# VectorE and TensorE in program order in the first stage of a two-layer adaLN kernel

## The chip, the cores and the metric

The kernel runs on one core of a Trainium2 chip. The time is the device time of one execution in microseconds (us), the median of three runs. A profile of one further execution shows every instruction.

## What is computed

Two layers follow each other on `x` of 8 batches, 512 tokens and 256 channels, all in float32. Each layer has an attention part and an expert part, and both are modulated (adaLN): shift, scale and gate come from a small product of `silu(c)`.

```python
h = _layernorm(x) * (1 + ca) + sa
x = x + ga * attention(h)
h = _layernorm(x) * (1 + cb) + sb
x = x + gb * experts(h)
```

In layer 0 the attention is a linear one with 16 heads of 64: `q` and `k` have one number a head, and running sums over the tokens replace the softmax.

```python
cos_KV = jnp.cumsum(cos_k * V, axis=1)
sin_KV = jnp.cumsum(sin_k * V, axis=1)
heads = cos_q * cos_KV + sin_q * sin_KV
denom = cos_q * cumsum(cos_k) + sin_q * cumsum(sin_k) + EPS
heads = heads / denom
out = jnp.einsum('deh,bthe->btd', W_O, heads)
```

Its experts are 4, two for each token, with `silu(x w1) * (x w3)` and `w2`. Layer 1 has a softmax attention among 16 positions of small heads, and 8 experts, one for each token.

## The kernel before

**The stages.** The batches of layer 0 are in two halves, `first` (0 to 3) and `second` (4 to 7). The first stage runs the attention of batches 0 to 3, routes their tokens to experts, makes the table of expert tiles (`table`), and begins the attention of batch 4. Then the expert tiles of the first half start (`line.run(m0, ...)`): from there on TensorE works on expert tiles (`up` L753, `down` L768), and the attention of later batches and of layer 1 is put between them.

**Attention of one batch (`attend0`).** Before a batch's steps, `prepare0(b)` makes its rows in three parts. The first is `norm_T`: `stats` on VectorE (four `bn_stats`, an ACT Sqrt at L185, a reciprocal and one Newton step), the normalised `xn` on ScalarE (L198), transposes on TensorE (L217), modulation on ScalarE (`hT`, L204), the product `pq` (L336), Tanh and four Sin on ScalarE. It then goes on with `before` on GpSimd, the products `pd` (L358, L359), the denominators on VectorE (L362 to L369), transposes (L372) and row copies on ScalarE (L376). The last part is one VectorE product (L379), and the rows are written to DRAM from GpSimd's queue. The steps of batch b call the parts of batch b+1 at j = 0, 3 and 5.

The batch itself has 8 steps j of two heads each (`heads0`). SyncE (SP) loads `ratio` and `factor`, rows spread over the partitions, in four DMAs of 256 KB (3 and 2 buffers). TensorE makes `pv` (L398). VectorE runs two scans (L404), a product (L407) and an addition (L409) to `hd`. After the eight steps `out0` multiplies by `W_O`: four tiles of 128 tokens, `poa` (L415), each of eight products over all `hd`. VectorE multiplies each tile by the gate (`ra`, L226) and GpSimd adds it to `x` (L227).

**Routing (`Moe.route`).** For a batch whose attention is done: `stats` and `normed` again, transposes (L499), logits `pl` (L504), transposes back (`prow`, L512), `z` on VectorE (L520), an Exp on ScalarE, two maxima with their indices (`first_max`), prefix sums, a product `pk` with a triangle (L562), slot positions (L575), and eight indirect DMAs from GpSimd's queue that scatter the rows to slots (L579). The generator stops five times on the way. `table` then counts the tiles.

**What sets the order.** The code is generators: `weave(main, side)` runs one piece of `side` after each piece of `main`. In the first stage, batch 0's steps are woven with loads and the modulation of layer 1 (`rest`), and those of batch b with the routing of batch b-1 and then the re-ordering of a weight (`wq_steps`, ScalarE copies). That is the program's order. It is not the order of the engines: the framework schedules the traced instructions and puts each engine's queue in the order in which it expects their inputs to be ready. At run time an engine's queue is worked through as written. Manual dependencies and `issue_after` are the only marks on that order.

PSUM has four buffers for `pv` and expert products (`ps_h`), two for `poa` (`ps_o`), and two for all small products and transposes (`ps_m`).

Of the kernel before, what the change touches and what calls it, by code (L numbers as in the profile page):

```python
# [9 lines left out]
F32 = mybir.dt.float32  # L10
# [18 lines left out]
def kernel(  # L29
# [99 lines left out]


# [3 lines left out]
    def modulation(l, c, wmod, mp):  # L134
# [4 lines left out]
        for n in range(3):  # L139
# [3 lines left out]
            for kk in range(KD):  # L143
                nc.tensor.matmul(pr[:B, :], sc[:, kk, :], wm[:, kk, :], start=(kk == 0), stop=(kk == KD - 1))
            rows = mp.tile([B, 2, D], F32, tag="rows", name=f"rows{l}_{n}", bufs=1)
            nc.vector.tensor_copy(rows.rearrange("b c d -> b (c d)"), pr[:B, :])
            for i in range(2):
                j = 2 * n + i
                if j % 3 == 1:
                    nc.vector.tensor_scalar(rows[:, i], rows[:, i], 1.0, None, ALU.add)  # L150
                elif j % 3 == 2:
                    sgn = mp.tile([B, D], F32, tag="sgn", name=f"sgn{l}_{j}", bufs=1)
                    nc.vector.tensor_scalar(sgn, rows[:, i], 0.0, 2.0, ALU.is_ge, ALU.mult)
                    mag = mp.tile([B, D], F32, tag="mag", name=f"mag{l}_{j}", bufs=1)
                    nc.scalar.activation(mag, rows[:, i], AF.Abs)
                    nc.vector.tensor_scalar(mag, mag, GATE_MIN, None, ALU.max)
                    nc.vector.scalar_tensor_tensor(rows[:, i], sgn, -1.0, mag, ALU.add, ALU.mult)
            by_channel = [i for i in range(2) if (2 * n + i) % 3 != 2]
            pm = ps_m([P, len(by_channel), KD, B], f"pmT{l}_{n}")
            for m, i in enumerate(by_channel):  # L160
                for k in range(KD):
                    nc.tensor.transpose(pm[:, m, k, :], rows[:, i, k * P : (k + 1) * P], ident[:B, :B])
            at = (0, 2, 3)[n]
            nc.vector.tensor_copy(modT[l][:, at : at + len(by_channel)], pm)
# [10 lines left out]
    def stats(b, nm):  # L175
# [3 lines left out]
        for t in range(NT):  # L179
            nc.vector.bn_stats(st[:, t, :], x[b][:, t, :])  # L180
            nc.vector.bn_aggr(mv[:, t, :], st[:, t, :])
        v = wk.tile([P, NT], F32, tag="var", name=f"var{nm}")
        nc.vector.tensor_scalar(v, mv[:, :, 1], LN_EPS, None, ALU.add)
        r = wk.tile([P, NT], F32, tag="rstd", name=f"rstd{nm}")
        nc.scalar.activation(r, v, AF.Sqrt)  # L185
        nc.vector.reciprocal(r, r)
        n = wk.tile([P, NT], F32, tag="newton", name=f"newton{nm}")
        nc.vector.scalar_tensor_tensor(n, r, -0.5, r, ALU.mult, ALU.mult)
        nc.vector.tensor_mul(n, n, v)
        nc.vector.scalar_tensor_tensor(r, n, 1.5, r, ALU.add, ALU.mult)  # L190
        return mv, r

    def normed(b, mv, r, dst, nm):

        sh = wk.tile([P, NT], F32, tag="sh", name=f"sh{nm}")
        nc.vector.scalar_tensor_tensor(sh, mv[:, :, 0], -1.0, r, ALU.mult, ALU.mult)
# [11 lines left out]
    def norm_T(l, b, dst):  # L208


        mv, r = stats(b, f"{l}_{b}")
        xn = wk.tile([P, NT, D], F32, tag="xn", name=f"xn{l}_{b}", bufs=1)
        normed(b, mv, r, xn, f"{l}_{b}")
        for k in range(KD):
            pt = ps_m([P, NT, P], f"pt{l}_{b}_{k}")
            for t in range(NT):
                nc.tensor.transpose(pt[:, t, :], xn[:, t, k * P : (k + 1) * P], ident)  # L217
# [5 lines left out]
    def residual(po, gate, b, t, name):  # L223

        tmp = wk.tile([P, D], F32, tag="tmp", name=name, bufs=2)
        nc.vector.tensor_mul(tmp, po, gate)  # L226
        nc.gpsimd.tensor_tensor(x[b][:, t, :], x[b][:, t, :], tmp, ALU.add)  # L227
# [101 lines left out]
    def prepare0(b):  # L329
# [4 lines left out]
        for t in range(NT):  # L334
            for k in range(KD):
                nc.tensor.matmul(  # L336
# [21 lines left out]
        nc.tensor.matmul(pd, tri, c, start=True, stop=False)  # L358
        nc.tensor.matmul(pd[:, 1:], ones, before, start=False, stop=True)  # L359
        ab = tr[:, :, 2]  # L360
        rd = ap.tile([P, NT, H], F32, tag="rd", name=f"rd{b}", bufs=1)
        nc.vector.tensor_mul(ab, sq, pd)  # L362
        nc.vector.tensor_add(rd, ab[:, :, 0, :], ab[:, :, 1, :])
        nc.vector.tensor_scalar(rd, rd, DEN_EPS * math.sin(2 * ALPHA), None, ALU.add)
        nc.vector.reciprocal(rd, rd)
        nc.vector.reciprocal(tr[:, :, 1], c)
        for i in range(2):
            nc.vector.tensor_mul(ab[:, :, i], sq[:, :, i], rd)
        nc.vector.tensor_mul(ab, ab, c)  # L369
        pt = ps_m([3 * 2 * H, NT, P], f"ptr{b}")  # L370
        for t in range(NT):
            nc.tensor.transpose(pt[:, t, :], tr[:, t].rearrange("p a i h -> p (a i h)"), ident)  # L372
# [6 lines left out]
        nc.vector.tensor_mul(rows[1][:, 1:], rows[1][:, 1:], rows[0][:, : S - 1])  # L379
# [5 lines left out]
    def heads0(b, j):  # L385
# [11 lines left out]
        for k in range(KD):  # L397
            nc.tensor.matmul(  # L398
                pv, wv_sb[:, k, j * P : (j + 1) * P], hTs[b][:, k, :],
                start=(k == 0), stop=(k == KD - 1),  # L400
            )
        u = ap.tile([P, 2, S], F32, tag="u", name=f"u{b}_{j}", bufs=2)
        for i in range(2):
            nc.vector.tensor_tensor_scan(  # L404
                out=u[:, i], data0=w[0][:, i], data1=pv, initial=0.0, op0=ALU.mult, op1=ALU.add
            )
        nc.vector.tensor_mul(u, u, w[1])  # L407
        hd = ap.tile([P, S], F32, tag="hd", name=f"hd{b}_{j}", bufs=9)
        nc.vector.tensor_add(hd, u[:, 0], u[:, 1])  # L409
        return hd  # L410

    def out0(b, t, hds, ga):
        po = ps_o(f"poa{b}_{t}")
        for j in range(NJ):
            nc.tensor.matmul(  # L415
                po, hds[j][:, t * P : (t + 1) * P], wo_sb[:, j, :], start=(j == 0), stop=(j == NJ - 1),
            )
        residual(po, ga, b, t, f"ra{b}_{t}")

    def attend0(b):  # L420

# [3 lines left out]
        for j in range(NJ):  # L425
            hds.append(heads0(b, j))
            if j in (0, 3, 5):
                next(nxt, None)
            yield
        for t in range(NT):  # L430
            out0(b, t, hds, ga)
        yield

    hTs = {}
# [10 lines left out]
    def first_max(v, E, m, o, name):  # L445


        nc.vector.tensor_reduce(m, v, AX.X, ALU.max)
        nc.vector.tensor_tensor(o, v, bcast(m, E), ALU.is_equal)
        nc.vector.tensor_mul(o, o, desc[:, :E].unsqueeze(1).to_broadcast([P, NT, E]))  # L450
        k = wk.tile([P, NT], F32, tag="rm", name=f"k{name}", bufs=4)
        nc.vector.tensor_reduce(k, o, AX.X, ALU.max)
        nc.vector.tensor_tensor(o, o, bcast(k, E), ALU.is_equal)

    class Moe:
# [19 lines left out]
        def route(self, i):  # L475
# [9 lines left out]
            h0 = ht[0]  # L485
            mv, r = stats(b, f"f{bm}")
# [9 lines left out]
            for k in range(KD):  # L496
                pt = ps_m([P, NT, P], f"ptr{bm}_{k}")
                for t in range(NT):
                    nc.tensor.transpose(pt[:, t, :], h0[:, t, k * P : (k + 1) * P], ident)  # L499
                by_channel(l, 2, k, b, hT[:, k], pt.rearrange("p t q -> p (t q)"))  # L500
            pl = ps_m([P, NT, E], f"pl{bm}")
            for t in range(NT):
                for k in range(KD):
                    nc.tensor.matmul(  # L504
# [3 lines left out]
            for t in range(0, NT, 2):  # L508
                pb = ps_m([P, 2, D], f"prow{bm}_{t}")
                for q in range(2):  # L510
                    for k in range(KD):
                        nc.tensor.transpose(  # L512
# [7 lines left out]
            nc.vector.tensor_tensor(z, pl, b_sb.unsqueeze(1).to_broadcast([P, NT, E]), ALU.add)  # L520
# [6 lines left out]
            if l == 0:  # L527
                s = wk.tile([P, NT], F32, tag="rs", name=f"s{b}")
                nc.vector.tensor_reduce(s, z, AX.X, ALU.max)
                nc.vector.tensor_tensor(z, z, bcast(s, E), ALU.subtract)  # L530
                nc.scalar.activation(z, z, AF.Exp)
                nc.vector.tensor_reduce(s, z, AX.X, ALU.add)
                nc.vector.reciprocal(s, s)
                nc.vector.tensor_mul(z, z, bcast(s, E))
                first_max(z, E, m[0], ch[0], f"a{b}")
                nc.vector.scalar_tensor_tensor(z, ch[0], -2.0, z, ALU.mult, ALU.add)
                first_max(z, E, m[1], ch[1], f"b{b}")
                now = wk.tile([P, NT, E], F32, tag="now", name=f"now{bm}", bufs=2)
                nc.vector.tensor_add(now, ch[0], ch[1])
                nc.vector.tensor_add(s, m[0], m[1])  # L540
                nc.vector.reciprocal(s, s)
                for c in range(C):
                    nc.vector.tensor_mul(ht[c][:, :, D + 1], m[c], s)
            else:
                nc.scalar.activation(z, z, AF.Exp, scale=-1.0)
                nc.vector.tensor_scalar(z, z, 1.0, None, ALU.add)
                nc.vector.reciprocal(z, z)
                first_max(z, E, m[0], ch[0], f"c{b}")
                now = ch[0]
                nc.vector.tensor_copy(ht[0][:, :, D + 1], m[0])  # L550

            pre = fp.tile([P, NT + 1, E], F32, tag=f"pre{E}", name=f"pre{bm}", bufs=3)
            if i == 0:
                nc.vector.memset(pre[:, 0], 0.0)
            else:
                nc.vector.tensor_copy(pre[:, 0], self.run_)
            for t in range(NT):
                nc.vector.tensor_add(pre[:, t + 1], pre[:, t], now[:, t])
# [3 lines left out]
            nc.tensor.matmul(pk, tri, now, start=True, stop=False)  # L562
            nc.tensor.matmul(pk, ones, pre[:, :NT], start=False, stop=True)
            yield
            rank = wk.tile([P, NT, E], F32, tag="rank", name=f"rank{bm}", bufs=2)
            nc.vector.tensor_tensor(
# [4 lines left out]
            for c in range(C):  # L571
                nc.vector.tensor_mul(at, ch[c], rank)  # L572
                p_ = fp.tile([P, NT], I32, tag=f"pos{c}", name=f"pos{c}_{bm}", bufs=3)
                with nc.allow_low_precision("whole numbers"):
                    nc.vector.tensor_reduce(p_, at, AX.X, ALU.add)  # L575
# [16 lines left out]
        def table(self):  # L592
# [3 lines left out]
            nc.tensor.matmul(pn, ones, self.run_, start=True, stop=True)  # L596
            n = wk.tile([P, E], F32, tag="cnt", name=f"cnt{nm}", bufs=1)
            nc.vector.tensor_copy(n, pn)
            past_ = fp.tile([1, E1], I32, tag="pasts", name=f"past{nm}", bufs=2)[:, :E]
            nc.vector.scalar_tensor_tensor(past_, n[0:1], 1.0, cbase[0:1, :E], ALU.add, ALU.add)  # L600
            self.past = past_
            cmp_ = wk.tile([P, E, TH], F32, tag="cmp", name=f"cmp{nm}", bufs=1)
            nc.vector.tensor_tensor(
# [3 lines left out]
            nc.vector.tensor_reduce(nt, cmp_, AX.X, ALU.add)  # L607
            upto = wk.tile([P, E, E], F32, tag="upto", name=f"upto{nm}", bufs=1)
            nc.vector.tensor_tensor(
# [3 lines left out]
            nc.vector.tensor_reduce(end, upto, AX.X, ALU.add)  # L613
            base = wk.tile([P, E], F32, tag="base", name=f"base{nm}")
            nc.vector.tensor_sub(base, end, nt)
            full = [P, J, E]

            def of_tile(v, op, rows, dst, name, weigh=None):

                t_ = wk.tile(full, F32, tag="past", name=f"{name}{nm}", bufs=1)  # L620
                nc.vector.tensor_tensor(
                    t_, bcast(rows[:, :J], E), v.unsqueeze(1).to_broadcast(full), op
                )
                if weigh is not None:
                    nc.vector.tensor_tensor(t_, t_, weigh.unsqueeze(1).to_broadcast(full), ALU.mult)
                nc.vector.tensor_reduce(dst, t_, AX.X, ALU.add)
# [4 lines left out]
            nc.vector.tensor_scalar(self.tab[:, 0], which, float(E - 1), None, ALU.min)  # L631
            nc.vector.tensor_scalar(nt, nt, -1.0, float(CAP), ALU.mult, ALU.add)
            skip = wk.tile([P, J], F32, tag="skip", name=f"skip{nm}", bufs=1)
            of_tile(end, ALU.is_ge, iota, skip, "rows", weigh=nt)
            nc.vector.tensor_add(skip, skip, iota[:, :J])
            nc.vector.tensor_scalar(self.tab[:, 1], skip, float(P), float(E * CAP * P), ALU.mult, ALU.min)

            lim = wk.tile([P, E], F32, tag="lim", name=f"lim{nm}", bufs=1)
            nc.vector.scalar_tensor_tensor(lim, base, float(P), n, ALU.mult, ALU.add)
# [3 lines left out]
            nc.vector.tensor_sub(self.used, self.used, skip)  # L643
            self.rest = fp.tile([P, JMAX], F32, tag="rest", name=f"rest{nm}", bufs=2)[:, :J]
            nc.vector.scalar_tensor_tensor(
# [5 lines left out]
        def keep(self, end):  # L651
# [3 lines left out]
            nc.vector.tensor_scalar(  # L655
# [8 lines left out]
            for t, v in zip(k, (self.tab, self.used, self.rest)):  # L664
                nc.vector.tensor_copy(t, v[..., over])
# [602 lines left out]
```

## Time and profile before

| | us |
|---|---|
| median of three runs | 2013.6 (2009.74 to 2014.16) |
| the profiled execution | 1998.39 |
| its span, first to last instruction | 1996.7 |
| PE busy in the span | 1757.0 (88%) |
| DVE busy | 1258.1 (63%) |
| ACT busy | 728.8 (37%) |
| POOL busy | 594.9 (30%) |
| first scan of batch 0 | at 40.7 |
| first scan of batch 4 | at 274.4 |
| first expert matmul | at 328.9 |

PE is TensorE, PEld its weight loads, DVE VectorE, ACT ScalarE, POOL GpSimd, SP SyncE; `SPq` is SP's queue of DMAs. A row of the timeline gives start, length, engine, line, operation, out <- in, and how many instructions it merges (`x4`); a float32 matmul counts as two. In square brackets stands the engine's idle time before it, and what ended that. A row of the waits gives who waited, for whom, the total in us, how often and the longest. Granted clock (`PEclk`) is in tenths of full speed in the slices, and as a fraction in the windows.

### The profile page before, as it was taken

How to read it: one execution, taken by the hardware profiler on the slowest of the kernel's cores; microseconds unless marked ns; L12 is line 12 of the kernel's file. 1: busy time of each engine (PE TensorE's matmuls, PEld its weight loads, DVE VectorE, ACT ScalarE, POOL GpSimd, SP SyncE). 2: the span in 40 equal slices, each digit the busy share in tenths (PEclk: the TensorE clock that was granted, in tenths of full speed). 3: DMA queues.
4: the chain of work that ended last, by engine and by line, in shares of the span. 5: the costliest groups of instructions: out<-in, count | busy, mean ns of one | idle time of the engine just before them, and what ended most of it. 6: DMA issues, size and time to landing. Idle time of an engine off the chain costs nothing. (4 is left out here: it accounts for less than half of the span.)

```text
span 1996.7 us, 32445 instructions
## 1 busy us (share of the span) xinstructions
PE 1757.0 (88%) x11336; PEld 1536.1 (77%) x11336; DVE 1258.1 (63%) x2200; ACT 728.8 (37%) x1384; POOL 594.9 (30%) x564
## 2 busy tenths in 40 slices
PE   6686776999999999989999999997969988898895
PEld 3354435888888889888999889897868877787784
DVE  4786886344433441235999999623499999986200
ACT  5052212231312212226343334622645646454221
POOL 1033132121121121233435444213345464433210
PEclk9797986999999999989999999998989999899898
DMA  7977777899898996896777668799644665579795
GB/s 225 213 206 204 181 185 252 238 315 301 260 307 276 310 332 224 315 323 214 240 246 230 215 229 280 239 320 312 201 132 144 208 202 181 188 241 330 254 348 168
DMA packets 328535, 488.60 MB, mean 245 GB/s; under 512 B 24016, under 2 KB 184048, under 8 KB 327728
## 3 DMA queue, kind: packets, MB, share of 16 engines
q1 hardware_dynamic: 313840, 445.17, 71.6%
q0 software_dynamic: 14528, 41.31, 5.6%
q8 instruction: 92, 1.51, 0.3%
q14 instruction: 75, 0.61, 0.1%
HBM read 446.40 MB, written 45.27 MB: 246 GB/s over the span
## 5 line engine op out<-in xcount | busy, mean ns | idle before, releaser
L753 PE MATMUL p<-xT,w 128*128 128x128 f32 x6144 | 767.5, 281 | 29.7 <-DMA w<-in_W_dram 16.3
L753 PEld LDWEIGHTS p<-xT,w 128*128 128x128 f32 x6144 | 747.0, 198 | 44.4 <-issue 20.1
L768 PE MATMUL po<-w_d,g 128*128 128x256 f32 x1952 | 477.8, 385 | 26.7 <-DVE g L760 16.8
L768 PEld LDWEIGHTS po<-w_d,g 128*128 128x128 f32 x1952 | 355.3, 193 | 78.8 <-DVE g L760 20.5
L783 POOL DMA_INDIRECT ys<-y,to x122 | 153.9, 1261 | 658.3 <-ACT xT L728 420.8
L758 ACT ACTIVATE g<-p 128x512 f32<-128x512 f32 x244 | 145.8, 598 | 462.8 <-PE p L753 432.8
L760 DVE TENSOR_TENSOR g<-g,p 128x512 f32<-128x512 f32 x140 | 95.8, 685 | 274.0 <-PE p L753 253.9
L404 DVE TENSOR_TENSOR_SCAN u<-ratio,pv 128x512 f32<-128x512 f32 x128 | 149.6, 1204 | 57.1 <-PE pv L398 51.4
L989 POOL TENSOR_TENSOR far<-q 128x1024 f32<-128x1024 f32 x64 | 133.1, 2081 | 120.2 <-DVE pr L1047 75.8
L398 PE MATMUL pv<-hT,wv_sb 128*128 128x512 f32 x256 | 138.1, 661 | 33.6 <-DVE u L404 27.5
L415 PE MATMUL poa<-wo_sb,hd 128*128 128x256 f32 x512 | 128.4, 399 | 20.2 <-DVE hd L409 19.7
L775 ACT ACTIVATE y<-po,xs 128x256 f32<-128x256 f32 x122 | 57.8, 473 | 235.8 <-PE po L768 193.2
L579 POOL DMA_INDIRECT hs<-ht,pos x96 | 113.1, 1179 | 93.3 <-DVE at L572 32.4
L415 PEld LDWEIGHTS poa<-wo_sb,hd 128*128 128x128 f32 x512 | 98.3, 198 | 54.2 <-DVE hd L409 33.3
L971 PE MATMUL pqk<-wq_sb,hTa 128*128 128x128 f32 x1024 | 124.8, 281 | 5.1 <-ACT q L978 4.7
L971 PEld LDWEIGHTS pqk<-wq_sb,hTa 128*128 128x128 f32 x1024 | 122.5, 198 | 6.7 <-ACT q L978 5.1
L1024 POOL TENSOR_TENSOR farv<-s,q 128x1024 f32<-128x1024 f32 x32 | 81.7, 2552 | 97.4 <-DVE pr L1021 84.4
L398 PEld LDWEIGHTS pv<-hT,wv_sb 128*128 128x128 f32 x256 | 48.5, 208 | 74.8 <-DVE u L404 35.1
L818 DVE TENSOR_TENSOR yl<-yl,gb 128x512 f32<-128x512 f32 (+1 forms) x24 | 20.6, 866 | 130.8 <-DMA yl<-ys 130.7
L1012 DVE TENSOR_TENSOR s<-s,far 128x1024 f32<-128x1024 f32 x64 | 89.4, 1400 | 0.7 <-POOL far L989 0.7
L758 ACT ACT_TABLE_LOAD x61 | 78.3, 1283 | 6.3 <-PE p L753 5.3
L407 DVE TENSOR_TENSOR u<-u,factor 128x1024 f32<-128x1024 f32 x64 | 78.1, 1220 | 1.4
(203 smaller groups left out, 2013.9 us busy)
## 6 DMA issues: line engine op xcount, KB each, us to landing
w<-in_w_dram SPq DMA_DIRECT2D x280, 512.0 KB, 5.6
w_d<-in_w_dram SPq DMA_DIRECT2D x140, 512.0 KB, 5.8
w<-in_W_dram SPq DMA_DIRECT2D x104, 512.0 KB, 6.0
w_d<-in_W_dram SPq DMA_DIRECT2D x104, 512.0 KB, 6.7
ratio<-rows SPq DMA_DIRECT2D x128, 256.0 KB, 6.7
factor<-rows SPq DMA_DIRECT2D x128, 256.0 KB, 6.4
xs<-hs SPq DMA_DIRECT2D x122, 129.0 KB, 3.4
yl<-ys POOLq DMA_DIRECT2D x32, 256.0 KB, 7.6
```

The costliest lines, as they stand in the source:

```text
L398: nc.tensor.matmul(pv, wv_sb[:, k, j * P : (j + 1) * P], hTs[b][:, k, :], start=(k == 0), stop=(k == KD - 1),)
L404: nc.vector.tensor_tensor_scan(out=u[:, i], data0=w[0][:, i], data1=pv, initial=0.0, op0=ALU.mult, op1=ALU.add)
L415: nc.tensor.matmul(po, hds[j][:, t * P : (t + 1) * P], wo_sb[:, j, :], start=(j == 0), stop=(j == NJ - 1),)
L579: ins = nc.gpsimd.indirect_dma_start(out=self.hs, out_offset=bass.IndirectOffsetOnAxis(ap=pos[c][:, t : t + 1], axis=0), in_=ht[c][:, t, : ...
L753: nc.tensor.matmul(p1[:, f * P : (f + 1) * P], ws[n][:, k, f * P : (f + 1) * P], u["xT"][:, k, :], start=(k == 0), stop=(k == KD - 1),)
L758: nc.scalar.activation(gq, pp[0], AF.Silu if l == 0 else AF.Gelu)
L760: nc.vector.tensor_mul(gq, gq, pp[1])
L768: nc.tensor.matmul(u["po"], u["g"][:, q * NF // 2 + f, :], u["w2"][q][:, f, :], start=(q == 0 and f == 0), stop=(q == 1 and f == NF // 2 - 1),
L783: ins = nc.gpsimd.indirect_dma_start(out=self.ys, out_offset=bass.IndirectOffsetOnAxis(ap=to, axis=0), in_=y, in_offset=None,).ins
L971: nc.tensor.matmul(pq[:, hh], hT[:, k, hb * 4 + hh].rearrange("p b r -> p (b r)"), wq_sb[:, k, i, gh].rearrange("p d w g -> p (d w g)"), s ...
L989: ins = nc.gpsimd.tensor_tensor(t, part(u, 0, d, True), part(u, 1, d, False), ALU.mult).ins
L1012: nc.vector.tensor_add(s, s, far[u, d])
```

## The change

1. A wrapper `Ordered` stands for VectorE (`vec`) and TensorE (`mat`). While it is on, every instruction that goes through it is pinned behind the one traced before it on its engine; this orders the queue and adds no wait of its own. It is on from batch 0's steps to three steps of batch 4 after the table. All VectorE and TensorE calls go through it (most lines of the diff are that).
2. `heads0` is split. `begin0` loads the rows and makes `pv`, and it is called one step ahead.
3. `out0` of batch b moves to steps 0 and 1 of batch b+1, two tiles each, behind the step's scans. `hd` has 10 buffers in place of 9.
4. `prepare0` has a further stop between `pd` and the denominators. Its parts are called at j = 0, 2, 3 and 5.
5. Routing in layer 0 stops twice before it begins and once after the Exp. The `wq_steps` are woven beside it from batch 1 on.
6. Around the table, steps of batch 4 and parts of batch 3's routing alternate as listed.
7. Four norms of layer 1 (`half == 1`) take their inverse root from a first guess by bits and three Newton steps on VectorE, in place of the ACT Sqrt, the reciprocal and one step.

```diff
+    class Ordered:
+        def __init__(self, engine):
+            self.engine, self.on = engine, False
+        def __getattr__(self, name):
+            issue = getattr(self.engine, name)
+            def call(*args, **kw):
+                ins = issue(*args, **kw)
+                if self.on:
+                    tc.keep_in_program_order(ins)
+                return ins
+            return call
+    vec, mat = Ordered(nc.vector), Ordered(nc.tensor)
...
-        nc.scalar.activation(r, v, AF.Sqrt)
-        nc.vector.reciprocal(r, r)
+        if alone:
+            half = r.bitcast(I32)
+            vec.tensor_scalar(half, v.bitcast(I32), 1, None, ALU.logical_shift_right)
+            with nc.allow_low_precision("a first guess"):
+                vec.tensor_scalar(half, half, -1.0, float(0x5F3759DF), ALU.mult, ALU.add)
+        else:
+            nc.scalar.activation(r, v, AF.Sqrt)
+            vec.reciprocal(r, r)
         n = wk.tile([P, NT], F32, tag="newton", name=f"newton{nm}")
-        nc.vector.scalar_tensor_tensor(n, r, -0.5, r, ALU.mult, ALU.mult)
-        nc.vector.tensor_mul(n, n, v)
-        nc.vector.scalar_tensor_tensor(r, n, 1.5, r, ALU.add, ALU.mult)
+        for _ in range(3 if alone else 1):
+            vec.scalar_tensor_tensor(n, r, -0.5, r, ALU.mult, ALU.mult)
+            vec.tensor_mul(n, n, v)
+            vec.scalar_tensor_tensor(r, n, 1.5, r, ALU.add, ALU.mult)
...
+        mat.matmul(pd, tri, c, start=True, stop=False)
+        mat.matmul(pd[:, 1:], ones, before, start=False, stop=True)
+        yield
         ab = tr[:, :, 2]
...
-    def heads0(b, j):
+    def begin0(b, j):
...
+        begun[b, j] = w, pv
+
+    def heads0(b, j):
+
+        w, pv = begun.pop((b, j))
...
     def attend0(b):
         ga = gate(0, 0, b, "ga", ap, 2)[:, 0]
         nxt = prepare0(b + 1) if b + 1 < B else iter(())
         hds = []
         for j in range(NJ):
+            if (b, j) not in begun:
+                begin0(b, j)
+            if j + 1 < NJ:
+                begin0(b, j + 1)
+            elif b + 1 < B:
+                begin0(b + 1, 0)
             hds.append(heads0(b, j))
-            if j in (0, 3, 5):
+            if j < 2 and pending:
+                out0(*pending[0], range(2 * j, 2 * j + 2))
+                if j:
+                    pending.pop()
+            if j in (0, 2, 3, 5):
                 next(nxt, None)
             yield
-        for t in range(NT):
-            out0(b, t, hds, ga)
-        yield
+        pending.append((b, hds, ga))
+        if b + 1 == B:
+            out0(*pending.pop(), range(NT))
+            yield
...
+            if l == 0:
+                yield
+                yield
             mv, r = stats(b, f"f{bm}")
...
                 nc.scalar.activation(z, z, AF.Exp)
+                yield
...
+    vec.on, mat.on = True, True
     for b in first:
-        drain(weave(attend0(b), chain(m0.route(b - 1), wq_steps) if b else rest))
+        drain(weave(weave(attend0(b), m0.route(b - 1)), wq_steps) if b else weave(attend0(b), rest))
         if b == 1:
             finite()
     drain(wq_steps)
-    drain(m0.route(HB - 1))
-    m0.table()
     a1 = chain(
...
-    for _ in range(7):
+    last = m0.route(HB - 1)
+    for f in (a1, a1, last, last, last, a1, last, a1):
+        next(f)
+    drain(last)
+    m0.table()
+    for _ in range(3):
         next(a1)
+    vec.on = mat.on = False
...
-            norm_T(1, half * HB + i, hT[:, :, :, i, :])
+            norm_T(1, half * HB + i, hT[:, :, :, i, :], alone=half == 1)
```

## Prediction, made before the changed kernel was run

> **What bounds the kernel now.** I read the busy tenths of the page first, to see which part of the span is not TensorE's; then the windows of that part; then who VectorE waits for there; then the timelines of VectorE, TensorE and ScalarE in it, for the durations.
>
> Busy tenths in 40 slices of 49.9 us:
>
> ```profile
> PE   6686776999999999989999999997969988898895
> DVE  4786886344433441235999999623499999986200
> PEclk9797986999999999989999999998989999899898
> ```
>
> Seven slices at the left are the first stage. TensorE is at 6 to 8 tenths, VectorE at 4 to 8, neither full; after it TensorE is near full almost to the end. The page's chain of work reaches back only to the last table (1846 us) and says nothing of this stage.
>
> Windows (columns: busy PE, PEld, DVE, ACT, POOL, then clock, DMA share, GB/s), from the first scan to the end of batch 3's steps, and from the first scan to the first expert matmul:
>
> ```profile
> 40.70:267.40 226.70, 170.15 (x576) 98.96 (x576) 177.45 (x354) 60.68 (x152) 53.56 (x78) 0.84 0.80 204
> 40.70:328.90 288.20, 202.23 (x699) 120.96 (x700) 224.90 (x491) 77.59 (x185) 71.43 (x108) 0.80 0.76 198
> ```
>
> VectorE is busy 224.9 of 288.2 us: 63 idle is all this stage can give on VectorE. What it waits for there:
>
> ```profile
> DVE stf L180 <- POOL x L227: 13.9, 11, 4.3
> DVE z L520 <- PE pl L504: 13.4, 4, 7.3
> DVE tr L362 <- PE pd L359: 7.9, 4, 4.0
> DVE ra L226 <- PE poa L415: 7.8, 7, 2.1
> DVE tr L366 <- ACT tr L348: 7.1, 3, 3.8
> DVE u L404 <- DMA ratio<-rows: 3.0, 1, 3.0
> ```
>
> These are hops to another engine and back, 58 us with the small ones. The order before is not the program's: scans of one batch lie among routing of another.
>
> Durations, from the timelines:
>
> ```profile
> 258.90 2.32 DVE L404 TENSOR_TENSOR_SCAN u<-ratio,pv 128x512 f32<-128x512 f32 x2
> 261.26 1.23 DVE L407 TENSOR_TENSOR u<-u,factor 128x1024 f32<-128x1024 f32 x1
> 262.52 0.69 DVE L409 TENSOR_TENSOR hd<-u 128x512 f32<-128x512 f32 x1
> 263.13 2.33 DVE L404 TENSOR_TENSOR_SCAN u<-ratio,pv 128x512 f32<-128x512 f32 x2
> 265.51 1.98 PE L398 MATMUL pv<-hT,wv_sb 128*128 128x512 f32 x4 [1.11 <-DVE u L404]
> 217.08 8.39 PE L415 MATMUL poa<-wo_sb,hd 128*128 128x256 f32 x36
> 109.54 1.75 PE L336 MATMUL pq<-wqk_sb,hT 128*128 128x32 f32 x14
> 309.07 3.20 PE L336 MATMUL pq<-wqk_sb,hT 128*128 128x32 f32 x14 [0.22 <-ACT hT L204]
> 172.66 2.06 ACT L198 ACTIVATE xn<-x,sh,rstd 128x256 f32<-128x256 f32 x4
> 164.09 1.45 ACT L204 ACTIVATE hTr<-ptr,modT 128x512 f32<-128x512 f32 x2 [0.57 <-PE ptr L499]
> ```
>
> One step j of attend0 costs VectorE 4.23 (258.90 to 263.13). A `pv` is 2.0 of TensorE. `poa` is 8.39/36 = 0.233 a record, 16 records a tile, so 3.73 a tile, 15 a batch. First scans of batches 0 and 4 are at 40.7 and 274.4: 233.7 for four batches, 58.4 each. From there to the last slot position of batch 3 (308.0) it is 33.6, and 20.9 more to the first expert matmul (328.9): scatter, landing, reload.
>
> **The change, part by part.** Times in one batch b of the steady state (1 to 3) count from its first scan, S.
>
> *VectorE's own work in program order.* Eight steps 33.9; four `ra` 1.6; two `stats` with their Newton step 6.4 (3.2 each, 4.65 to 7.84 in the trace); denominators and `row` product 3.3; `z` 0.6; the two maxima and prefix of routing 4.6; rank and positions 0.9. Sum 51.3. The tiny dependent operations follow each other every 0.2 us; before, scans are pushed in between, and busy time is only 177.45/4 = 44.4 a batch. Program order so gives up some 4 to 5 a batch of overlap that the trace shows.
>
> *Waits removed.* Routing one step later lets the POOL addition land (13.9), the split of prepare0 lets `pd` and the sines land (7.9, 7.1), and `exp` gets a step. These go.
>
> *Waits added: TensorE's order.* At j = 0 VectorE runs scans to S+4.2, `ra` 0 and 1 to S+5.1 (TensorE has their products ready but for the last record), then `stats` of b+1 to S+8.3. From there TensorE is chained: `xn` 2.1, transposes 0.3, `hT` 1.5, transposes and hand-over 0.3, `pq` 1.8, so S+14.3. Only behind it in TensorE's order stand `pv` of step 2 (2.0, S+16.3), `poa` tile 2 (3.7, S+20.0) and tile 3 (3.7, S+23.7). VectorE has meanwhile only step 1 (to S+12.5), and then `ra` 2 and `ra` 3, which are pinned ahead of step 2's scans. It ends `ra` 3 at S+24.1: 10.8 of wait a batch. Queued behind are all scans of the batch; who waits for them is the rest of the stage. TensorE can't fill the gap either, since the next `pv` is behind the same instructions.
>
> *Smaller ones.* At j = 3 transposes of `tr`, of routing, `pl` and `prow` follow each other through two PSUM buffers and ScalarE copies (1.78, 1.45, 2 x 0.59), so `z` at j = 4 waits 1.6 for `pl`, and step 5's `pv`, behind `prow`, costs 2.6. Wait in all 15.0, batch 51.3 + 15.0 = 66.3 against 58.4: +7.9, three batches +24.
>
> *The clock.* TensorE now idles from S+4.3 to S+8.6, beyond the 2.9 to 3.4 us after which the trace has `pv` at 3.78 for 1.98 and `pq` at 3.20 for 1.75. By the rows, transposes and `pq` lose 0.8 + 1.45 a batch. [...] As it lies in the chain of the 10.8, I take 1.7, four times: +7; range 0 to +9.
>
> *Batch 0.* No `poa`, no routing: eight steps 33.9, stats 3.2, denominators 3.3, a wait for `pv` of step 2 behind `pq` of 3.7, and three modulation steps that VectorE now walks in order with TensorE and ScalarE (some 4.3 each at 0.7 copy, 1.8 to 3.6 products, 0.4 Abs, 0.3 transposes): 57 against 61.2, so -4. Its output product moves to batch 1. If the weight rows of the last modulation land late, up to +4.
>
> *Batch 4 up to the table.* 24.1 as above, `stats` of batch 3 with a wait for POOL's addition 4, step 2 4.2, step 3 with denominators 6.9, `z` 0.6, `exp` now bare with its table load 2, maxima 4.6, `pk` 0.6, rank 0.9: 48 against 33.6, +14. The table comes after that as before; three further steps lie beside the 20.9 of scatter, as three did before.
>
> *SP's and POOL's queues.* Loads for step j+1 are written in step j: the same four of 256 KB, with the same buffers, so they start when the same scans free them (5 to 6 us to landing, within the 7.2 of one buffer's turn). 0; with the buffers late, 3 as in the row above. The write of `rows` stays at j = 5. ScalarE, POOL and SP are not pinned; wq copies (1.2 a step) beside each step of batch 1 may delay `xn`: 0 to +4, taken 0.
>
> *Newton in place of Sqrt*, four norms near 900 us: a Sqrt and up to two table loads of 1.28 leave ScalarE, seven operations of 0.2 join VectorE. TensorE's idle there for `xn` is 0.5 in all: 0, bounds -3 to +3. The rest of the program keeps its order free; a shift may fall well or badly, -6 to +6, taken 0.
>
> Sum: 24 + 7 - 4 + 14 = **+41**. The profiled execution took 1998.4 (span 1996.7), so 2039; the median of the timed runs is 2013.6, 15 above it, and I add to that: 2055.
>
> **The rivals.**
> - *A, the order stalls as laid out*: 2055, own range 2028 to 2078. For it: the chain is made of durations of the trace, and `ra` 3 has no way round. Against it: before has 14 us hops too, and some were in unlike places.
> - *B, TensorE runs far enough ahead that `ra` 2 and 3 find their tiles ready*: the 10.8 and the 1.7 of the clock go, four times, 41 - 50 = -9, so 2005; if the small waits (1.6 + 2.6, four times) go too, -26, 1988. Against it: `pq` stands in front, and it needs `hT`, and that VectorE's own `sh`. This is the fast side; it would also hold where the pinning is not strict and only the earlier inputs count.
> - *C, half of each*: `poa` is pulled partly into the gap, or before's bubble (149 to 173 us) was worse than its repeat: 8 or so, within 2010 to 2028.
>
> The slow side is one mechanism, `ra` 2 and 3 in VectorE's order waiting for tiles that stand behind `pq` in TensorE's. It costs 12.5 with its cold clock, four times; the rest of the sum is -9, so from 9/4 = 2.3 us a batch on the change loses.
>
> **How the numbers follow.** A 0.66, C 0.09 (slower but for 0.02), B 0.25. Differences within 0.2% (4 us) can't be told from none here. Of B 0.02 and of C 0.02 fall within that. Faster 0.23, same 0.04, slower 0.73. Range: from 1996, between B's two values, to 2078; some 0.12 lie below and 0.05 above.
>
> **What would show it.** The wait `ra <- poa` grows from 7.8 to 35 or more in the window; `stf <- POOL x` nearly goes; scans of steps 1 and 2 stand about 16 us apart, those of 5 to 8 about 4 to 9; the first expert matmul moves from 329 to about 370, and the rest shifts with it. If `ra <- poa` stays near 8 and the first expert matmul comes before 329, B is right and A's chain was wrong.

## The result and the profile after

| | before | after |
|---|---|---|
| median of five runs, us | 2010.89 (2003.53 to 2014.16) | 2087.73 (2079.75 to 2091.69) |
| span of the profiled execution | 1996.7 | 2078.1 |
| first scan of batch 0 | 40.73 | 38.72 |
| first scan of batch 1 | 101.89 | 109.07 |
| first scan of batch 2 | 173.13 | 189.41 |
| first scan of batch 3 | 219.42 | 262.04 |
| first scan of batch 4 | 274.42 | 336.52 |
| last slot position of batch 3 | 308.0 | 390.6 |
| first expert matmul | 328.9 | 417.6 |
| from there to the end of the span | 1667.8 | 1660.5 |

The change makes the kernel slower: ratio 1.0372, 95% interval 1.0353 to 1.0391. All of it lies ahead of the first expert matmul (+88.7); what follows is 7.3 shorter. The profiled executions differ by 81.4, the medians by 76.8; the sums below compare profile with profile.

The busy tenths of the changed kernel, 40 slices of 52 us:

```profile
PE   5567667499999999998999999999887999799895
DVE  4557666835345442223599999951569999997100
PEclk7676777699999999999999999999999999899898
```

The first stage now takes eight slices in place of seven, and the granted clock in it is 6 or 7 tenths where it was mostly 7 to 9. The windows from the first scan to that of batch 4, and to the first expert matmul (columns as before):

```profile
38.72:336.52 297.80, 187.38 (x594) 120.87 (x595) 193.85 (x384) 78.13 (x176) 43.35 (x74) 0.72 0.60 159
38.72:417.60 378.88, 234.60 (x738) 151.40 (x738) 250.22 (x527) 97.90 (x211) 69.19 (x111) 0.71 0.58 157
```

VectorE is idle 128.7 us of the longer stretch; before it was 63. Its largest waits in 38 to 440 us (all wrapped calls carry the wrapper's line, L140; go by the names):

```profile
DVE ra L140 <- PE poa L140: 58.9, 10, 11.6
DVE u L140 <- PE pv L140: 22.4, 6, 6.9
DVE rows L140 <- PE pmod L140: 13.6, 2, 12.0
DVE z L140 <- PE pl L140: 12.1, 3, 4.0
```

`stf <- POOL x`, the largest before, is not in the list any more. In its place stands the output product. TensorE and then VectorE at step 1 of batch 1:

```profile
123.80 2.81 PE L140 MATMUL pt<-ident,xn 128*128 128x128 f32 x8 [4.72 <-ACT xn L224]
...
127.63 3.19 PE L140 MATMUL pq<-wqk_sb,hT 128*128 128x32 f32 x14 [0.33 <-ACT hT L230]
130.64 3.76 PE L140 MATMUL pv<-hT,wv_sb 128*128 128x512 f32 x4
134.19 8.13 PE L140 MATMUL poa<-wo_sb,hd 128*128 128x256 f32 x32
```

```profile
115.66 0.42 DVE L140 TENSOR_TENSOR ra<-poa,ga 128x256 f32<-128x256 f32 x1 [2.29 <-PE poa L140]
119.12 0.42 DVE L140 TENSOR_TENSOR ra<-poa,ga 128x256 f32<-128x256 f32 x1 [3.03 <-PE poa L140]
...
126.66 0.69 DVE L140 TENSOR_TENSOR hd<-u 128x512 f32<-128x512 f32 x1
138.98 0.42 DVE L140 TENSOR_TENSOR ra<-poa,ga 128x256 f32<-128x256 f32 x1 [11.63 <-PE poa L140]
142.43 0.42 DVE L140 TENSOR_TENSOR ra<-poa,ga 128x256 f32<-128x256 f32 x1 [3.03 <-PE poa L140]
```

This is the chain of the prediction: `hd` of the batch before is done, and the first two `ra` have freed the two `poa` buffers at 116.1 and 119.5 us. So tiles 2 and 3 lack nothing from there on, and TensorE stands idle for 4.72 us until 123.8. But in its order these tiles stand behind `pt`, `pq` and `pv`, and VectorE's next scans stand behind the last two `ra`. The wait repeats in every batch with 12.1 to 14.7 us. Everything in the chain ahead of `poa` runs at about half rate (`pq` 3.19 for 1.75, `pv` 3.76 for 1.98; in batch 2 the granted clock is 0.50 in `pt` and `pq` and 0.57 in that `pv`).

### The profile page after: what moved, and what is told of

Its sections match the earlier page's. It is cut to its first block, busy times and chain, and to the rows that moved or that the text cites. A ratio compares the mean times of both kernels' runs of the same rounds, so it can differ in the third digit from the quotient of the medians.

```text
span 2078.1 us, 32519 instructions
## 1 busy us (share of the span) xinstructions
PE 1780.1 (86%) x11336; PEld 1559.0 (75%) x11336; DVE 1273.0 (61%) x2228; ACT 729.0 (35%) x1379; POOL 592.2 (28%) x564
## 4 chain that ended last, share of the span: by engine, by line
PE 25%; DVE 15%; issue 4%; DMA 4%; ACT 3%; POOL 0%; SPq 0%; ACTq 0%; POOLq 0%; DVEq 0%
PE p L140 12%; PE po L140 8%; DVE s L140 5%; DVE o L140 3%; PE pqk L140 2%; DVE pr L140 2%; DMA w<-in_W_dram 2%; DVE sum L140 1%; PE pao L140 1%; DVE mx L140 1%; PE pl L140 1%; DVE g L140 1%; DMA yl<-ys 1%; ACT owT L1132 1%; PE pxs L140 0%
## 5 line engine op out<-in xcount | busy, mean ns | idle before, releaser
L140 PE MATMUL p<-xT,w 128*128 128x128 f32 x6144 | 762.8, 281 | 28.9 <-DMA w<-in_W_dram 16.3
L140 PEld LDWEIGHTS p<-xT,w 128*128 128x128 f32 x6144 | 743.3, 197 | 42.5 <-issue 17.8
L140 PE MATMUL po<-w_d,g 128*128 128x256 f32 x1952 | 480.0, 386 | 28.3 <-DVE g L140 20.9
L140 PEld LDWEIGHTS po<-w_d,g 128*128 128x128 f32 x1952 | 354.6, 193 | 79.8 <-DVE g L140 25.3
L140 DVE TENSOR_TENSOR g<-g,p 128x512 f32<-128x512 f32 x140 | 95.7, 684 | 295.8 <-PE p L140 247.4
L140 DVE TENSOR_TENSOR_SCAN u<-ratio,pv 128x512 f32<-128x512 f32 x128 | 149.2, 1206 | 85.7 <-PE pv L140 52.8
L140 PE MATMUL pv<-hT,wv_sb 128*128 128x512 f32 x256 | 146.0, 712 | 0.0
L630 POOL DMA_INDIRECT hs<-ht,pos x96 | 107.2, 1117 | 110.4 <-DVE at L140 48.8
L140 PE MATMUL pqk<-wq_sb,hTa 128*128 128x128 f32 x1024 | 124.7, 281 | 5.1 <-ACT q L1034 4.7
L140 PEld LDWEIGHTS pqk<-wq_sb,hTa 128*128 128x128 f32 x1024 | 122.4, 198 | 6.9 <-ACT q L1034 5.1
L140 PE MATMUL poa<-wo_sb,hd 128*128 128x256 f32 x512 | 118.8, 388 | 0.9 <-DVE ra L140 0.7
L140 PEld LDWEIGHTS poa<-wo_sb,hd 128*128 128x128 f32 x512 | 99.5, 196 | 24.2 <-issue 9.2
L140 DVE TENSOR_TENSOR pr<-s,q 128x1024 f32<-128x1024 f32 x96 | 116.1, 1211 | 0.1
L140 DVE TENSOR_REDUCE o<-pr 128x64 f32<-128x1024 f32 x96 | 115.3, 1209 | 0.0
L140 DVE TENSOR_TENSOR yl<-yl,gb 128x512 f32<-128x512 f32 (+1 forms) x24 | 20.7, 865 | 129.6 <-DMA yl<-ys 129.5
L140 PEld LDWEIGHTS pv<-hT,wv_sb 128*128 128x128 f32 x256 | 56.2, 232 | 52.8 <-issue 52.0
L140 DVE TENSOR_TENSOR s<-s,far 128x1024 f32<-128x1024 f32 x64 | 89.1, 1395 | 0.7 <-POOL far L1045 0.7
```

Of the source, the lines that this page charges most:

```text
L140: ins = issue(*args, **kw)
L630: ins = nc.gpsimd.indirect_dma_start(out=self.hs, out_offset=bass.IndirectOffsetOnAxis(ap=pos[c][:, t : t + 1], axis=0), in_=ht[c][:, t, : ...
```

## The experiments

The theory: two in-order queues that wait for each other, at a few named places. Its rivals: the moves alone cost it; Newton does; the cold clock does; keeping order costs by itself, wherever the parts stand. Ratios are to the kernel before, with 95% intervals.

**Which part of the change.** Each kernel is the changed one with one line different.

```diff
-    vec.on, mat.on = True, True
+    vec.on, mat.on = False, False     # e1_free
+    vec.on, mat.on = True, False      # e2_vec
+    vec.on, mat.on = False, True      # e3_mat
...
-            norm_T(1, half * HB + i, hT[:, :, :, i, :], alone=half == 1)
+            norm_T(1, half * HB + i, hT[:, :, :, i, :], alone=False)      # e4_sqrt
```

Neither engine kept in order (the moves alone):

> The changed program with the pinning off on both engines; all else as changed. Theory (order): the loss is head-of-line waiting, ra 2 and 3 and z behind instructions that TensorE and VectorE are not free to pass. Then it goes with the pinning: 1990 to 2020 us, first expert matmul at 315 to 335, ra<-poa under 12 us. Rival (moves): the later output product, the later routing and the bare steps cost it themselves: then 2060 to 2090 stays.

VectorE alone:

> Only VectorE pinned, TensorE free. Theory (order), with TensorE's queue as the worse half: TensorE may put pv and the output tiles ahead of pq, so 2010 to 2040. If VectorE's own fixed order is the loss (tiny operations one after another, no scans between), it stays at 2060 to 2090. Rival (moves): 2060 to 2090 too.

TensorE alone:

> Only TensorE pinned, VectorE free. Theory (order): pv of step 2 still stands behind pq, but VectorE may take its scans ahead of ra 2 and 3; of the 14.6 us a batch at step 1 about 7 go, and the tiny operations mingle with scans again: 2030 to 2060. Rival (moves): 2060 to 2090.

Both, with the Sqrt back:

> The changed kernel with the four norms back on the Sqrt; all else as changed. The part behind the first expert matmul is 7.3 us shorter after the change (1660.5 for 1667.8). If Newton is the cause, this runs 2 to 7 us longer than the changed kernel's 2087.7; if the state at the hand-over is (more of batch 4 done), it is within 2 of it.

| | median | ratio |
|---|---|---|
| neither | 2024.1 | 1.0055 (1.0041 to 1.0070) |
| VectorE | 2017.6 | 1.0028 (1.0015 to 1.0041) |
| TensorE | 2037.8 | 1.0123 (1.0087 to 1.0159) |
| both (the change) | 2087.7 | 1.0372 (1.0353 to 1.0391) |
| both, Sqrt | 2087.9 | 1.0387 (1.0360 to 1.0413) |

The moves cost some 11 us, a little more than expected (2024.1 for at most 2020, and the first expert matmul at 359.8 for at most 335). Either order alone adds no more than 14 to that. Both together cost 77. So the loss is in the meeting of the two orders. With TensorE free (e2_vec), its queue has 26 records of `poa` ahead of `pq`, and `ra <- poa` falls from 58.9 to 2.7:

```profile
169.22 5.88 PE L140 MATMUL poa<-wo_sb,hd 128*128 128x256 f32 x26 [0.34 <-DVE ra L140]
...
178.27 1.75 PE L140 MATMUL pq<-wqk_sb,hT 128*128 128x32 f32 x14 [0.26 <-ACT hT L230]
```

With VectorE free (e3_mat) it falls to 4.8, though other waits grow (`stf <- POOL x` to 36.7). Of Newton nothing can be told from these intervals, which leave some 5 us either way.

**Where in TensorE's order.** In e6_norm1 the next batch's preparation is called one step later, so that `pt` and `pq` stand behind `poa` of tiles 2 and 3. In e7_pv2 the call of `pv` is a function of its own, made two steps ahead. e8_both has both.

```diff
-            if j in (0, 2, 3, 5):
+            if j in (1, 3, 4, 5):              # e6, e8
...
+            for n in (j, j + 1, j + 2):        # e7, e8: values0 makes pv
+                at = (b, n) if n < NJ else (b + 1, n - NJ)
+                if at[0] < B and at not in asked:
+                    asked.add(at)
+                    values0(*at)
```

> The changed kernel, with the four parts of the next batch's preparation called one step later each (1, 3, 4, 5 in place of 0, 2, 3, 5), so that its transposes and pq stand behind the output products of tiles 2 and 3 in TensorE's order. If ra 2 and 3 behind pq are the main stall, ra<-poa falls from 58.9 us to under 25, part of it comes back as u<-pv (the values of step 3 now stand behind pq), and the time is 2040 to 2060. If the stall is only one of many of the same size, it moves on whole: 2075 to 2095.

Measured 2045.1 us (1.0164, 1.0127 to 1.0201). That is 42 us back with one tuple. VectorE's waits in 38 to 440 us of e6_norm1:

```profile
DVE u L140 <- PE pv L140: 19.7, 7, 6.9
...
DVE ra L140 <- PE poa L140: 10.4, 7, 3.0
```

`ra <- poa` falls by 48.5, and `u <- pv`, expected to grow, does not.

> The changed kernel, with the products pv of a scan written two steps ahead in place of one; the loads stay one ahead. The waits u<-pv (22.4 us) go; ra 2 and 3 stay behind pq and wait one pv longer or shorter. By the order theory the time is 2060 to 2075; if pv is no bound of its own, 2080 to 2095.

Measured 2067.4 us (1.0264, 1.0232 to 1.0295), within what was expected. In the same stretch `u <- pv` falls from 22.4 to 2.7, `ra <- poa` stays at 60.7.

> The changed kernel with both of these edits: preparation one step later and pv two steps ahead. If the two places of TensorE's order (ra behind pq, pv behind pq and prow) are what the change loses beyond VectorE's own program order, VectorE waits for TensorE only at z and the modulation, and the time is 2005 to 2030, the first expert matmul at 340 to 365. If pinning both engines loses by itself, wherever the parts stand, 2050 to 2090.

Measured 2041.2 us (1.0128, 1.0095 to 1.0162), between the two cases and in neither. The waits for TensorE are indeed small (`ra <- poa` 17.6, `u <- pv` 2.7), but a new one stands in their place, which the expectation had not seen. VectorE and POOL in e8_both:

```profile
DVE ra L140 <- POOL x L253: 26.7, 5, 9.8
```

```profile
251.42 1.04 POOL L551 TENSOR_SCALAR ht<-slot 128x1 f32<-128x1 f32 x4 [6.37 <-DMA hs<-ht,pos]
252.54 2.77 POOL L253 TENSOR_TENSOR x<-x,ra 128x256 f32<-128x256 f32 x4
```

`ra` has two buffers, freed by POOL's additions to `x`. In POOL's queue those stand behind eight scatters (234.3 to 245.1 us) and behind the next `ht` columns, which wait until the scatters out of the same buffer have landed. The stall had moved to the third in-order queue.

**POOL's queue, and the modulation's loads.** e10_mod issues the loads of the second modulation (`cT`, the first two `wm`) four steps earlier, in the changed kernel. e12_order has e8's two edits, these loads, and POOL kept in order for the additions and the columns.

```diff
+        if early:
+            there = [load(0), load(1)]
+            yield
...
-        nc.gpsimd.tensor_tensor(x[b][:, t, :], x[b][:, t, :], tmp, ALU.add)
+        pool.tensor_tensor(x[b][:, t, :], x[b][:, t, :], tmp, ALU.add)
...
-                    nc.gpsimd.tensor_scalar(
+                    pool.tensor_scalar(
```

> The changed kernel, with the loads of the second modulation's inputs (cT and the first two weight blocks wm) issued four steps earlier in batch 0, in SP's queue ahead of the scan inputs of later steps; all computation stays where it is. If VectorE's 12.0 us of wait for pmod at 99.3 us is those loads standing behind scan inputs in SP's queue, it goes and the time is 2072 to 2079. If those inputs then land later and the scans wait in its place: 2082 to 2092.

Measured 2084.0 us (1.0335, 1.0302 to 1.0368), in the second case: less was gained than hoped. The 12.0 us of wait for `pmod` at the end of batch 0 are gone, but batch 0 is only 4.0 shorter (66.3 for 70.35). The rest came back as waits for `ratio` (3.4), for the second `pmod` (3.3) and for `rows` to be free of its write (5.8 in place of 2.7).

> The kernel with preparation one step later and pv two steps ahead, and two more edits: POOL too keeps the program's order in the residual additions and the slot columns (where VectorE waited 26.7 us for POOL, whose additions stood behind columns that wait for a scatter to land), and the modulation's inputs are loaded earlier. If VectorE's order itself costs little and the loss is these waits, 2041 falls by about 20 and 8 to 2005 to 2020, and VectorE waits less than 35 us in all in the stage. If VectorE's program order costs by itself (no tiny operations beside scans): 2025 to 2040.

Measured 2021.6 us (1.0028, 1.0013 to 1.0042), just above what was expected. The batches now take 60.6, 64.8, 61.4 and 59.7. No wait of VectorE stands out any more, but they still sum to 65 us up to the first expert matmul, where under 35 was expected. The largest ones of e12_order in the same stretch, those in the expert tiles left out:

```profile
DVE ra L140 <- PE poa L140: 18.8, 9, 3.8
DVE u L140 <- DMA ratio<-rows: 17.0, 4, 8.5
DVE rstdf L140 <- ACT rstdf L218: 11.0, 5, 4.5
```

So 66 of the 77 us are the price of a few places in three queues (TensorE's, POOL's and SP's), while VectorE, TensorE and part of POOL stay in program order. What POOL's order and the early loads gave here was not separated. Order by itself is not what costs most: with it kept, about 0.3% is left.

**The cold clock.** Products whose results nothing reads are put at the two places where TensorE stands idle, ahead of `pt` at step 1 and ahead of `tr` at step 4.

```diff
+            if j == 0 and mat.on:
+                keep_warm(b, 9)         # e9_warm2: 5
+            if j == 3 and mat.on:
+                keep_warm(b, 20)        # e9_warm2: 11
```

> The changed kernel, with extra TensorE products whose results nothing reads: 9 ahead of the norm of the next batch's transposes at step 1, 20 ahead of the denominators' part at step 4. They change no order among the real products; they only keep TensorE from standing idle so long. If the prediction's wait was undersized because TensorE, idle for 4 to 11 us at a time, runs the whole chain at half rate (pq 3.2 instead of 1.8, pv 3.8 instead of 2.0, poa 8.1 for 32 records instead of 7.4), then pq and pv go back to 1.8 and 2.0, the granted clock of the stage rises from 0.72 to 0.85 or more and the time falls to 2045 to 2060. If order alone sets the waits, the time stays at 2080 to 2095, or rises because the extra products stand in front of real ones.

Measured 2100.8 us (1.0441, 1.0403 to 1.0479). The products took 0.88 each and overran the gaps, so the total decides nothing. Their trace is of use. With the granted clock at 1.00 (batch 2), it is 4.1 us from the last `xn` to the Tanh behind `pq`, for 5.5 in the changed kernel, and from the transposes of `tr` to `pl` it is 5.7 for 8.1. The `pv` behind `pq` stayed slow all the same (3.4 to 3.6).

> The earlier run with extra products put 7.9 and 17.3 us of them into gaps of about 6 and 11.5 us, so they stood in the way of the real ones. Here the same with 5 and 11 products (4.4 and 9.6 us), so that they end before the real work is ready; nothing reads their results. In that earlier run pt and pq took 1.04 and 2.16 in place of 2.81 and 3.84, and the chain from tr to pl 5.7 in place of 8.1. If that is what the cold clock costs, each batch wins about 2.6 at step 1 and 2.3 at z: four times, 2065 to 2075. If the waits are set by order alone: 2080 to 2095.

Measured 2084.8 us (1.0350, 1.0317 to 1.0382), which cannot be told from the change itself. The four batches take 294.2 in place of 297.8, 0.9 each. The last filler stands in front of `pk` in the tail (`rank <- pk` 5.7), and the tail takes 57.5 in place of 54.0, which gives all of that back. The clock did not stay up even so. Windows of e9_warm2 in batch 2: `pt`, `pq`, the `pv` behind it, and `poa`:

```profile
196.90:199.14 2.24, 1.75 (x8) 0.94 (x8) 2.21 (x3) 1.82 (x4) 1.91 (x4) 1.00 1.00 322
199.57:203.25 3.68, 3.65 (x17) 3.51 (x17) 1.76 (x2) 1.90 (x2) 2.41 (x5) 0.50 0.40 104
203.25:206.47 3.22, 3.22 (x5) 1.43 (x6) 0.00 (x0) 2.95 (x7) 0.21 (x1) 0.55 1.04 225
206.47:213.38 6.91, 6.91 (x34) 6.08 (x32) 0.42 (x1) 0.96 (x1) 1.22 (x3) 1.00 0.09 19
```

The column before the last two is the granted clock: full at `pt`, half at `pq`, though from 183.9 us on TensorE had stood idle for no longer than 1.64 us at a time. Nor does busy time bring it back at once. In the changed kernel, behind the gap of 11.5 us at step 4 of batch 2, it stayed at half for 9.7 us (`tr` to `prow`), with TensorE busy in 8.1 of them:

```profile
230.90:238.90 8.00, 6.39 (x29) 5.79 (x30) 4.02 (x4) 3.29 (x5) 0.63 (x1) 0.50 0.70 164
238.90:240.60 1.70, 1.70 (x10) 1.70 (x10) 0.52 (x3) 0.58 (x1) 0.00 (x0) 0.50 0.29 61
```

The clock is a part of the loss. In batch 2 of e5_warm, with `pt` and `pq` at 1.00 in place of 0.50, `ra` of tile 2 waited 8.09 us for `poa` in place of 9.03. In batch 1 of e9_warm2, with the five products ahead of `pt`, it waited 8.63 in place of 11.63: 3.0 us for this place. For the place at step 4 there is only the chain of e5_warm, 2.3 us shorter. A way to keep the clock up in every batch was not found.

**The hand-over.** From the last slot position to the first expert matmul it is 27.1 us after, 20.9 before. SP's queue in the changed kernel:

```profile
406.17 1.66 SPq L737 DMA_DIRECT2D hs<-hs  x2
411.97 0.65 SPq L418 DMA_DIRECT2D ratio<-rows  x1
413.44 1.24 SPq L771 DMA_DIRECT2D xs<-hs  x2
```

The first load of expert rows (`xs`) stands behind a `ratio` load that waits for a scan of batch 4. e11_hand takes two of the three steps of batch 4 out of that place.

```diff
-    for _ in range(3):
-        next(a1)
+    next(a1)
     vec.on = mat.on = False
```

> The changed kernel, with one step of batch 4 in place of three written between the table and the first expert tile; the other two go to where the free order has them, beside the expert products. If the first load of the expert rows stands behind scan inputs in SP's queue that wait for these steps' scans, the time from the last slot position to the first expert product falls from 27.1 to about 21 us and the total to 2076 to 2083; the two steps (8.5 us of VectorE, 4 of TensorE) may come back beside the experts. If SP's queue isn't it: 2084 to 2095.

Measured 2092.5 us (1.0378, 1.0335 to 1.0421). The hand-over falls to 19.3 (395.6 to 414.9), as expected. But the total, expected at 2076 to 2083, cannot be told from that of the change, and in the profile the stretch from the first expert matmul to the end is 1679.1 in place of 1660.5. The cause of the 6 us is shown; no gain shows in the total.

**What remains.** e14_vecpool is e12_order with TensorE free; e13_vecmod is e2_vec with the modulation's loads early.

```diff
-    vec.on, mat.on, pool.on = True, True, True
+    vec.on, mat.on, pool.on = True, False, True      # e14
...
-    vec.on, mat.on = True, True
+    vec.on, mat.on = True, False                     # e13, with the early loads
```

> Only VectorE keeps the program's order (2017.6 in the run that did that alone, with 16.7 us of waits for pmod), and the modulation's inputs are loaded earlier in batch 0. In the fully ordered kernel that edit took 12 us of wait away and gave 8 back to scan inputs and the modulation's own hops. If the same holds here: 2011 to 2016. If the whole wait goes: 2000 to 2008, faster than before. If VectorE is late for other reasons: 2017 to 2022.

> The kernel of 2021.6 us with all repairs (preparation one step later, pv two ahead, POOL in order, modulation loads early), with TensorE's order left free. If TensorE's kept order still cost what remains (18.8 us of ra<-poa, 4.4 of z<-pl), the time falls to 2003 to 2012. If what remains is VectorE's own order, its tiny operations no longer between the halves of scans: 2015 to 2025.

Measured 2015.2 us (0.9994, 0.9977 to 1.0011) and 2015.4 us (1.0012, 0.9996 to 1.0028): neither can be told from the kernel before. For e13 that is the first case. For e14 it is the low end of the case that VectorE's order is what remains; but its interval overlaps that of e12_order, so the runs do not say which order the last 0.3% belongs to. With TensorE free, VectorE's program order costs nothing that the total shows, and gains nothing either. None of the versions is faster than the kernel before.

## Why the prediction was right or wrong

The direction and the mechanism were right, the size was not: +81.4 from profile to profile in place of +41. Two steps of the sum failed most. Batch 0 was put at -4, with nothing for late weight blocks of the modulation, and measured +9.2; VectorE waited 12.0 for them. The small waits of each later batch (`z` and the `pv` of step 5) were put at 1.6 + 2.6 from warm durations, and measured 4.0 + 4.1, 12 us in three batches. Hand-over, tail and `ra` 0 and 1 of batch 1, each 5 to 6 us, make up most of the rest. By terms:

| term of the sum | forecast | measured |
|---|---|---|
| first scan of batch 0 | 0 | -2.0 |
| batch 0 | -4 | +9.2 |
| batches 1 to 3, with their clock | +29 | +54.9 |
| batch 4 to the last slot position, with its clock | +16 | +20.4 |
| hand-over | 0 | +6.2 |
| the rest, with Newton | 0 | -7.3 |

- **The 10.8 of `ra` 2 and 3, and 1.7 of clock.** Right in sum. Measured 14.7, 12.1, 13.3 and 13.6 in batches 1 to 4, against 12.5. No run shows the 1.7: with extra products ahead of `pt`, 0.9 of the wait went in batch 2 of e5_warm and 3.0 in batch 1 of e9_warm2. e6_norm1 shows that this place is the main one: 42 us. Rival B fails for the reason given against it: `pq` stands in front.
- **VectorE's own work of 51.3 a batch.** Right: batches 1 to 3 took 227.5, less 71.4 of waits, so 52.0 each.
- **"Smaller ones": 1.6 for `z` and 2.6 for `pv`.** Mis-sized, the largest error of the steady batches. `z` waited 4.0, `pv` 4.1 in the mean. The working took warm durations for the transposes, `pl` and `prow`; they ran at half rate behind a second gap of 11.5 us at step 4, which the clock term had left out. At full clock the chain to `pl` is 2.3 shorter (e5_warm), which by its length is nearly the whole error of `z`. Behind the second gap of batch 2 the clock stayed at half for 9.7 us (windows in the part on the cold clock). In this stage, with small products on the critical chain, the clock has to be in the sum, once for each gap.
- **`ra` 0 and 1 "ready but for the last record".** Right in batches 2 to 4, wrong in batch 1, where 5.3 was waited: TensorE had only just finished the modulation at the end of batch 0, and `pv` and `poa` came behind it.
- **Batch 0: -4.** Wrong, by 13.2: 3.2 at the first `pv` behind `pq` (6.9 for 3.7), 8.9 in the three modulation steps (21.8 for 12.9), and about 1 elsewhere. The text had the case of late weight rows, at "up to +4", and took 0. The `wm` loads stood behind scan inputs in SP's queue (issued at 89.8 us, behind `ratio` at 86.1 and `factor` at 87.9), and VectorE, now bound to the program's order, waited 12.0 for their product with nothing else allowed. With these loads early (e10_mod) the three steps take 14.6, near the forecast, but the scans ahead of them wait 3.4 more for `ratio`, so that 4.0 of batch 0 is won.
- **SP's queue: 0.** Right for the scans, wrong for the hand-over: +6.2, an `xs` load behind a `ratio` load. The step said when loads become free to start, not who stands behind them.
- **The tail, +14.** Nearly right: 54.0 for 48. Of the 6, 1.7 stood in the sum apart, as its clock term; the Exp took 3.6 for 2, and the step-1 chain about 1 more than its clock term. The rest stays open.
- **The baseline.** 58.4 a batch was a mean over four with batch 0's 61.2; batches 1 to 3 of before take 57.5. That is 2.7 of the gap.
- **Newton: 0.** Nothing speaks against it: without Newton (e4_sqrt) the stretch behind the first expert matmul is the same 1660 us, and the totals cannot be told apart. What made this stretch 7.3 shorter stays open. From profile to profile of the kernels here it varies from 1656 to 1679; in e10_mod, where nothing behind the first expert matmul is changed, it is 1671.3. So 7.3 may be no effect at all.

What was to show the prediction right did so: `ra <- poa` over 35 (58.9), `stf <- POOL x` gone, `ra` far behind step 1 (the scans of steps 1 and 2 stand 18.1 to 19.7 apart, expected 16). The first expert matmul at 417.6 for 370 is where the missing terms add up.

## What to carry to other kernels

When two engines are both bound to a written order, look for every place where the first one's wait is for something that the second has ready but holds behind work that needs the first. Here such a place cost 12.1 to 14.7 us in every batch, and moving one call by one step brought 42 us back. After each repair read the waits again, the third queue included: here the stall that was taken away in TensorE's queue came out in POOL's (`ra <- POOL x`, 26.7 us in e8_both).

## What the runs showed of the hardware that was not expected

- TensorE's granted clock fell to 0.50 with no idle stretch over 1.64 us (e9_warm2, windows above), and in e5_warm it was 0.52 in a `pv` that followed 3.7 us of small transposes and `pq` with gaps of 0.43 and 0.26 us. In the kernel before, which the prediction read as slow after 2.9 to 3.4 us, four records of `poa` follow a gap of 3.10 us twice: at 66.4 us they took 1.13, at 70.6 us 2.07. So in these runs the length of the idle gap alone does not tell when the clock falls.
- Small products did not bring the clock back: it stayed at 0.50 for 9.7 us of which TensorE was busy in 8.1 (230.9 to 240.6 us of the changed kernel).
- The `pv` right behind `pq` took 3.3 to 3.8 us in the changed kernel, 3.64 and 3.39 with extra products (batch 2 of e5_warm and e9_warm2), in place of 1.9 to 2.0. It is not so behind all small products: at 111.6 us of the kernel before one behind the routing's transposes took 1.88.
- GpSimd's eight scatters take 10.8 us of its queue (234.3 to 245.1 in e8_both), and the rows they read were free only 6.4 us after the last of them.
